# The last stage of a two-layer convolution kernel: which units come first, how far the projection runs ahead, and who issues the last stores

## The chip, the cores and the metric

The kernel runs on one core of one Trainium2 chip. The metric is device time in microseconds (us): the median of 3 executions of the whole kernel. The profile is of one execution; its span counts from the first to the last instruction. A core has five engines that the text names: TensorE (PE, with its weight loads shown apart as PEld), VectorE (DVE), ScalarE (ACT), GpSimd (POOL) and SyncE (SP, which here only issues DMAs). Each takes its own instructions in program order and they meet through semaphores. Results of TensorE land in PSUM; everything else lies in SBUF; x and the output lie in HBM.

## The reference, cut to what matters

The input x is one image of 384 channels by 192 x 192 pixels in float32. Two layers are added to it in turn:

```python
# layer 0: group norm, 1x1 products to q, k, v, 2x2 max, 3x3 depthwise, channel attention, GELU,
#          each pixel repeated to 2x2, 1x1 projection
x = x + _L0_conv_ref(_gn(x), w_qkv, b_qkv, w_dw, b_dw, w_proj, b_proj, temperature, a1, a2, a3, a4)
# layer 1: group norm, sign, a shift along the row that depends on the channel, 1x1 product with signs
x = x + _L1_conv_ref(_gn(x), weight, bias)

def _L1_conv_ref(x, weight, bias):            # cut
    xb, wb = sign(x), sign(weight)
    shifted = ...                             # channel c reads w + dx(c), dx between -3 and 3
    return einsum('bchw,oc->bohw', shifted, wb) + bias
```

The second group norm only decides signs, so of its statistics the kernel needs the mean of each group: `sign(x - mean)`. That mean is a mean over the whole image, so no sign can be taken before layer 0's attention is finished everywhere.

## The kernel before: the parts that matter

The image is worked on in 24 units of 8 rows. One unit of x is a tile of 128 partitions x 3 channel tiles x 1536 pixels, 2304 KB. The results of attention (`chunk`) are kept in SBUF, 4 units to a chunk, 6 chunks. Chunks and units of x share a pool of 8 slots (`big`); two single slots, `early` and `more`, are opened when other data is gone. So as the last stage begins, 6 slots hold chunks and 4 hold units of x. As the projections of a chunk's four units are done, its slot takes a unit.

In the last stage each unit goes through four steps:

- `summed` (`projected`): TensorE multiplies the attention result by the projection weights, 3 float32 matmuls for each of 3 output tiles m; VectorE adds product, bias and x in two instructions (even and odd rows) for each m;
- `signed`: ScalarE takes signs, 6 half-tiles, GpSimd moves some channels to their shifts;
- `finished`: TensorE multiplies the signs by the sign weights, 12 fp8 matmuls for each m; VectorE adds them to x in two instructions for each m;
- `stored`: a DMA to HBM, and into the freed slot the load of a later unit.

```python
    def projected(ps, u, m):
        xt = kept[u]
        o = chunk[u // UC][:, :, u % UC * PPX : (u % UC + 1) * PPX]
        x5 = xt.rearrange("p t (i a j b) -> p t a i j b", a=2, b=2, j=WP)
        for t in range(CT):
            nc.tensor.matmul(ps, wpr[:, t, m * P : (m + 1) * P], o[:, t, :], start=(t == 0), stop=(t == CT - 1))
        yb = ps.rearrange("p (i j) -> p i j", j=WP).unsqueeze(3).to_broadcast([P, PR, WP, 2])
        for r in range(2):
            nc.vector.scalar_tensor_tensor(x5[:, m, r], yb, bpr[:, m : m + 1], x5[:, m, r], ALU.add, ALU.add)
    ...
        with tc.manual_schedule():                       # end of the stage before; FIRST = (19, 18)
            ...
            for m in range(CT):
                projected(pqkv.tile(...)[:, :PPX], FIRST[0], m)
            attention(NAB - 1)
            projected(pqkv.tile(...)[:, :PPX], FIRST[1], 0)
            nc.vector.tensor_reduce(om, osum, AX.X, ALU.add)
            projected(pqkv.tile(...)[:, :PPX], FIRST[1], 1)
            ps = psp.tile([P, P], F32, name="p3ps")[:NG, :1]
            for t in range(CT):
                nc.tensor.matmul(ps, wg1[:, t], om[:, t : t + 1], start=(t == 0), stop=(t == CT - 1))
            nc.vector.tensor_scalar(gm, ps, -1.0 / (GRP * NPX), bg1, ALU.mult, ALU.add)
            projected(pqkv.tile(...)[:, :PPX], FIRST[1], 2)
            ps = psp.tile([P, P], F32, name="p3ps")[:, :CT].unsqueeze(2)
            spread(ps, gm)
            nc.vector.tensor_add(nmean1, nmean0, ps[:, :, 0])          # the mean, negative
    att.close()

    with end:
        more, sp = opened("p5x1", 1), opened("p5s", 1)
        pyp, psp = opened("p5py", 2, space=PSUM), opened("p5ps", 3, space=PSUM)
        ...
        ahead = [*FIRST, NU - 1, *(u for u in order if u // UC == FIRST[0] // UC and u not in FIRST)]
        order = [*ahead, *(u for u in order if u not in ahead)]        # 19, 18, 23, 17, 16, 22, 21, 20, 15, ...

        def signed(i):
            xt, sg = kept[order[i]], signs[i % NSIGN]                  # NSIGN = 3
            for k in range(2 * CT):
                ...
                nc.scalar.activation(..., AF.Sign, bias=nmean1[p, t : t + 1], saturate=False)
                moved(sg, t, h)                                        # GpSimd
                if i > 1 and k == min(2 * (i - 2), CT):
                    stored(i - 2)

        def finished(i, m):
            ...
            for r0 in range(0, UR, 4):
                ps = psp.tile([P, 2, 512], F32, name="l1ps")
                ...                                                    # 6 fp8 matmuls
                nc.vector.scalar_tensor_tensor(blk, ps[:, :, : 2 * W], bl1[:, m : m + 1], blk, ALU.add, ALU.add)
            if i + 2 >= NU:
                nc.sync.dma_start(ov[u, :, m], xt[:, m])

        def stored(i):
            ...
            n = 1 if i < CT else CT
            for t in range(0, CT, n):
                nc.scalar.dma_start(ov[u][:, t : t + n], xt[:, t : t + n])
            if todo:
                v = todo.pop(0)                                        # refill the slot
                for t in range(0, CT, n):
                    nc.sync.dma_start(xt[:, t : t + n], xv[v][:, t : t + n])
                kept[v] = xt

        with tc.manual_schedule():
            v = todo.pop(0)
            kept[v] = unit(v, more, parts=CT)
            for i in range(4):
                for m in range(CT):
                    summed(i, m)
                if i < 2:
                    signed(i)
            for i in range(NU):
                for m in range(CT):
                    if 1 < i < NU - 2:
                        summed(i + 2, m)
                    finished(i, m)
                if i + 2 < NU:
                    signed(i + 2)
```

`manual_schedule` means that each engine gets its instructions in just this order.

Of the kernel before, what the change touches and what calls it, by code (L numbers as in the profile page):

```python
# [10 lines left out]
F32 = mybir.dt.float32  # L11
# [5 lines left out]
ALU = mybir.AluOpType  # L17
# [130 lines left out]
def conv_preact_kernel(ctx: ExitStack, tc: tile.TileContext, a: dict, out: bass.AP):  # L148
# [406 lines left out]
    def opened(name, bufs, **kw):  # L555
        return end.enter_context(tc.tile_pool(name=name, bufs=bufs, reuse_waits="tile", **kw))

    def projected(ps, u, m):

        xt = kept[u]  # L560
        o = chunk[u // UC][:, :, u % UC * PPX : (u % UC + 1) * PPX]
        x5 = xt.rearrange("p t (i a j b) -> p t a i j b", a=2, b=2, j=WP)
        for t in range(CT):
            nc.tensor.matmul(  # L564
                ps,
                wpr[:, t, m * P : (m + 1) * P],
                o[:, t, :],
                start=(t == 0),
                stop=(t == CT - 1),
            )  # L570
        yb = ps.rearrange("p (i j) -> p i j", j=WP).unsqueeze(3).to_broadcast([P, PR, WP, 2])
        for r in range(2):
            nc.vector.scalar_tensor_tensor(x5[:, m, r], yb, bpr[:, m : m + 1], x5[:, m, r], ALU.add, ALU.add)  # L573

    chunk = []
    with ExitStack() as vs:
        wp = vs.enter_context(tc.tile_pool(name="p4w", bufs=1, side="right", reuse_waits="tile"))
        scratch = vs.enter_context(ExitStack())
        p3 = right("p3", stack=scratch)
        vs.enter_context(products_of_x)  # L580
        pool = padded(wp, CT)
        done, steps = 0, None

        def weights(name):
            wl = wp.tile([P, CT, C], F32, name="wl")
            tc.keep_in_program_order(nc.scalar.dma_start(wl, a[name].rearrange("(t p) o -> p t o", p=P)))
            return wl

        def attention(g):

            c, b = divmod(g, CPX // ABLK)
            cols = slice(b * ABLK, (b + 1) * ABLK)
            pss = [po.tile([P, ABLK], F32, name="ops") for _ in range(NP)]
            for t in range(CT):
                for p in range(NP):
                    rows = slice(p * Q, (p + 1) * Q)
                    nc.tensor.matmul(  # L597
                        pss[p][:PAIR],
                        aT[rows, t, p * PAIR : (p + 1) * PAIR],
                        chunk[c][rows, t, cols],  # L600
                        start=(t == 0),
                        stop=(t == CT - 1),
                    )
            for p, ps in enumerate(pss):
                for t in [p] if p < CT else range(CT):
                    src, to = (slice(0, PAIR),) * 2 if p < CT else (slice(t * Q, (t + 1) * Q), slice(PAIR, P))
                    nc.scalar.activation(chunk[c][to, t, cols], ps[src], AF.Gelu, accum_out=osum[to, t, g : g + 1])

        for u in range(NU):
            xt = kept.pop(NU + u) if NU + u in kept else unit(u)  # L610
            if u == NU - 1:
                kept[u] = xt
                for i, f in enumerate(FIRST):
                    kept[f] = unit(f, big if i else early)
            if u % UC == 0:
                chunk.append(big.tile([P, CT, CPX], F32, name="chunk", tag="big"))
            lo, hi = rows(u)
            first = PR * u - 2 + lo
            last = first + hi - lo
            for m in range(CT):  # L620
                parts = []
                for c in range(first // CR, last // CR + 1):
                    r0, r1 = max(first, c * CR), min(last, c * CR + CR - 1)
                    parts.append(
                        (chunk[c][:, m, (r0 - c * CR) * WP : (r1 + 1 - c * CR) * WP], r0 - first, r1 + 1 - r0)
                    )
                qkv_unit(pqkv, xt, u, 2 * CT + m, pool[m], parts)
                if m == 0 and u == UC:

                    wl = weights("w_projG").rearrange("p t (g c) -> p t g c", c=GRP)  # L630
                    tc.keep_in_program_order(nc.vector.tensor_reduce(wg1, wl, AX.X, ALU.add))
                if m == 0 and u == UC + 1:
                    tc.keep_in_program_order(nc.scalar.activation(wb, weights("weightT"), AF.Sign, saturate=False))
                if u == 0 and m == CT - 1:
                    gathered()
                    po = vs.enter_context(tc.tile_pool(name="p4o", bufs=NP, space=PSUM))
                    psp = vs.enter_context(tc.tile_pool(name="p3ps", bufs=1, space=PSUM))
                    bg = psp.tile([P, P], F32, name="p3ps")[:NG, :1]
                    group_sums(bg, bpr.unsqueeze(2))
                    nc.vector.tensor_scalar_mul(bg1, bg, -1.0 / GRP)  # L640
                if u >= TOPK and steps is None:
                    steps = softmaxes(p3, psp)
                if steps:
                    if next(steps, 1):
                        steps = ()
                        scratch.close()
                        early = opened("p5x0", 1)
                elif steps == () and done < NAB - HOLD and (done + 1) * ABLK <= first * WP:
                    attention(done)
                    done += 1  # L650
        with tc.manual_schedule():

            assert done == NAB - HOLD
            for g in range(done, NAB - 1):
                attention(g)
            for m in range(CT):
                projected(pqkv.tile([P, 512], F32, name="qkv")[:, :PPX], FIRST[0], m)
            attention(NAB - 1)
            projected(pqkv.tile([P, 512], F32, name="qkv")[:, :PPX], FIRST[1], 0)
            nc.vector.tensor_reduce(om, osum, AX.X, ALU.add)  # L660
            projected(pqkv.tile([P, 512], F32, name="qkv")[:, :PPX], FIRST[1], 1)
            ps = psp.tile([P, P], F32, name="p3ps")[:NG, :1]
            for t in range(CT):
                nc.tensor.matmul(ps, wg1[:, t], om[:, t : t + 1], start=(t == 0), stop=(t == CT - 1))
            nc.vector.tensor_scalar(gm, ps, -1.0 / (GRP * NPX), bg1, ALU.mult, ALU.add)
            projected(pqkv.tile([P, 512], F32, name="qkv")[:, :PPX], FIRST[1], 2)
            ps = psp.tile([P, P], F32, name="p3ps")[:, :CT].unsqueeze(2)
            spread(ps, gm)
            nc.vector.tensor_add(nmean1, nmean0, ps[:, :, 0])  # L669

    att.close()


    with end:
# [10 lines left out]
            return ts[p, at : at + UR * pitch].rearrange("p (r w) -> p r w", w=pitch)[:, :, :n]  # L685

        order = [u for c in reversed(range(NCH)) for u in reversed(range(c * UC, (c + 1) * UC))]
        ahead = [*FIRST, NU - 1, *(u for u in order if u // UC == FIRST[0] // UC and u not in FIRST)]
        order = [*ahead, *(u for u in order if u not in ahead)]
        left = [UC] * NCH  # L690
        todo = [u for u in order if u not in kept]
# [1 line left out]
        def summed(i, m):  # L693

            u = order[i]
            if i >= len(FIRST):
                projected(pyp.tile([P, PPX], F32, name="yps"), u, m)
            if m < CT - 1:
                return
            left[u // UC] -= 1  # L700
            if not left[u // UC] and todo:
                v = todo.pop(0)
                kept[v] = unit(v)

        def moved(sg, t, h):

# [20 lines left out]
        def signed(i):  # L727

            xt, sg = kept[order[i]], signs[i % NSIGN]
            for k in range(2 * CT):  # L730
# [7 lines left out]
                    saturate=False,  # L738
                )
                moved(sg, t, h)  # L740
                if i > 1 and k == min(2 * (i - 2), CT):
                    stored(i - 2)

        def finished(i, m):
# [3 lines left out]
            for r0 in range(0, UR, 4):  # L748
                ps = psp.tile([P, 2, 512], F32, name="l1ps")
                for j in range(2):  # L750
                    for t in range(CT):
# [4 lines left out]
                            start=(t == 0),  # L756
                            stop=(t == CT - 1),
                        )
                blk = xt[:, m, r0 * W : (r0 + 4) * W].rearrange("p (j n) -> p j n", j=2)
                nc.vector.scalar_tensor_tensor(  # L760
                    blk, ps[:, :, : 2 * W], bl1[:, m : m + 1], blk, ALU.add, ALU.add
                )
            if i + 2 >= NU:
                nc.sync.dma_start(ov[u, :, m], xt[:, m])

        def stored(i):


            u = order[i]
            xt = kept.pop(u)  # L770
            n = 1 if i < CT else CT
            for t in range(0, CT, n):
                nc.scalar.dma_start(ov[u][:, t : t + n], xt[:, t : t + n])
            if todo:
# [6 lines that stand above are left out]
# [6 lines left out]
                    signed(i)  # L787

            for i in range(NU):
                for m in range(CT):  # L790
                    if 1 < i < NU - 2:
                        summed(i + 2, m)
                    finished(i, m)
                if i + 2 < NU:
                    signed(i + 2)
# [72 lines left out]
```

## Time and profile before

| what | value |
|---|---|
| time, median of 3 (lowest, highest) | 2256.28 us (2255.89, 2258.26) |
| span of the profiled execution | 2254.6 us |
| mean granted TensorE clock | 0.968 |
| PE busy over the span | 2090.4 us (93%) |
| DVE busy | 1902.2 us (84%) |
| ACT busy | 819.7 us (36%) |
| POOL busy | 211.3 us (9%) |
| DMA moved | 300.30 MB, mean 133 GB/s |

In the page's picture of 40 slices the first 3 are statistics of x, about 31 are the two passes of layer 0, and the last 5 to 6 are the stage that is changed:

```
PE   1039999999999999999999999999999999999998
DVE  4667888888888888888888888986788888889998
ACT  4542222222222222222222222225333233397885
DMA  9962222232222222222223212105221312279997
```

Each digit is a busy share in tenths. In the last slices PE, DVE and the DMA engines all stand at 9: three resources are near their limit at once there, whereas before it PE stands at 9, DVE at 8 and the DMA at 2. The places where the change acts are the slice where the digits of DMA climb from 2 to 9 and the last one.

### The profile page before, as it was taken

What the parts mean: (1) busy time and instruction counts of PE and PEld (TensorE: products, weight loads), DVE (VectorE), ACT (ScalarE), POOL (GpSimd) and SP (SyncE); (2) the same over time, 40 slices, a digit from 0 to 9 for tenths busy, and PEclk for the clock granted to TensorE, in tenths of its full rate; (3) what the DMA queues carried; (4) which work ended last, traced back from release to release, by engine and by line L of the source; (5) the groups of instructions that cost most, each with busy time, mean ns of one, the idle gap of its engine ahead of it and who ended that gap; (6) DMA issues with size and microseconds to landing.
All of it is one profiled execution on the core that took longest, in us unless ns stands there. A gap on an engine that the chain in (4) does not pass through costs nothing.

```text
span 2254.6 us, 19480 instructions
## 1 busy us (share of the span) xinstructions
PE 2090.4 (93%) x6135; PEld 991.7 (44%) x6135; DVE 1902.2 (84%) x3267; ACT 819.7 (36%) x1418; POOL 211.3 (9%) x338
## 2 busy tenths in 40 slices
PE   1039999999999999999999999999999999999998
PEld 0014444444444444444444444443444444455554
DVE  4667888888888888888888888986788888889998
ACT  4542222222222222222222222225333233397885
POOL 0000000000000000000000000000000000086775
PEclk7559999999999999999999999999999999999999
DMA  9962222232222222222223212105221312279997
GB/s 397 418 277 62 65 64 70 66 105 67 70 63 67 71 73 96 71 67 63 70 67 94 77 35 85 53 11 210 84 84 42 113 55 84 84 296 394 424 425 308
DMA packets 208759, 300.30 MB, mean 133 GB/s; under 512 B 162032, under 2 KB 164880, under 8 KB 208656
## 3 DMA queue, kind: packets, MB, share of 16 engines
q1 hardware_dynamic: 197968, 243.46, 30.5%
q10 hardware_dynamic: 10688, 55.61, 6.0%
q8 instruction: 48, 0.79, 0.1%
q14 instruction: 55, 0.45, 0.1%
HBM read 213.68 MB, written 56.62 MB: 120 GB/s over the span
## 4 chain that ended last, share of the span: by engine, by line
PE 79%; DVE 11%; DMA 6%; ACT 2%; issue 1%; ACTq 0%; POOL 0%; SPq 0%; POOLq 0%; DVEq 0%
PE qkv L331 64%; DMA xt<-in_x_dram 6%; PE l1ps L752 5%; PE yps L564 5%; DVE chunk L356 5%; PE gram L415 3%; DVE pooled L338 2%; PE ops L597 2%; DVE dw L356 1%; ACT signs L733 1%; DVE xt L760 1%; ACT chunk L354 0%; ACT pooled L347 0%; DVE xt L573 0%; DMA small<-in_small_dram 0%
## 5 line engine op out<-in xcount | busy, mean ns | idle before, releaser
L331 PE MATMUL qkv<-xt,wq 128*128 128x512 f32 x3888 | 1684.0, 594 | 4.1 <-DVE pooled L338 3.3
L331 PEld LDWEIGHTS qkv<-xt,wq 128*128 128x128 f32 x3888 | 736.7, 190 | 925.6 <-issue 825.3
L356 DVE SCALAR_TENSOR_TENSOR dw<-pooled,small,dw 128x384 f32<-128x384 f32 (+2 forms) x1152 | 708.7, 615 | 118.8 <-ACT dw L354 93.6
L338 DVE TENSOR_REDUCE pooled<-qkv 128x128 f32<-128x512 f32 x648 | 442.3, 684 | 71.8 <-PE qkv L331 71.5
L356 DVE SCALAR_TENSOR_TENSOR chunk<-pooled,small,chunk 128x384 f32<-128x384 f32 (+3 forms) x696 | 369.7, 545 | 73.2 <-ACT chunk L354 55.5
L358 ACT COPY pooled<-pooled 128x196 f32<-128x196 f32 x207 | 73.7, 356 | 762.6 <-DVE dw L356 542.5
L347 ACT ACTIVATE pooled<-pooled,small 128x384 f32<-128x384 f32 x216 | 133.0, 616 | 405.8 <-DVE pooled L338 389.3
L733 ACT ACTIVATE signs<-xt,nmean 64x1536 fp8e4<-64x1536 f32 x144 | 226.5, 1573 | 47.7 <-PE yps L564 25.6
L752 PE MATMUL l1ps<-signs,wb 128*128 128x384 fp8e4 x864 | 152.6, 326 | 5.4 <-POOL signs L725 5.1
L760 DVE SCALAR_TENSOR_TENSOR xt<-l1ps,small,xt 128x768 f32<-128x768 f32 x144 | 138.8, 1008 | 4.1 <-issue 3.2
L564 PE MATMUL yps<-chunk,wpr 128*128 128x384 f32 x396 | 138.2, 487 | 1.8 <-DVE nmean L669 1.4
L573 DVE SCALAR_TENSOR_TENSOR xt<-yps,small,xt 128x768 f32<-128x768 f32 x132 | 128.0, 1012 | 12.9 <-PE yps L564 5.0
L276 DVE BATCH_NORM_STATS2 room<-xt 128x6 f32<-128x512 f32 x144 | 88.1, 676 | 49.1 <-DMA xt<-in_x_dram 49.1
L227 POOL MEMSET pooled<- 128x196 f32 x9 | 2.4, 265 | 1327.9 <-DVE dw L356 1310.5
L752 PEld LDWEIGHTS <-wb 128*128 128x128 fp8e4 x864 | 83.7, 97 | 78.1 <-issue 19.6
L438 ACT ACTIVATE sq<-dw 128x384 bf16<-128x384 f32 (+2 forms) x144 | 75.3, 523 | 117.5 <-DVE dw L356 117.5
L198 PE MATMUL gsps<-sums,small 128*32 128x2 f32 x6 | 0.5, 196 | 125.0 <-DVE sums L292 125.0
L354 ACT ACTIVATE dw<-pooled,small 128x384 f32<-128x384 f32 (+2 forms) x144 | 100.5, 698 | 2.2
L564 PEld LDWEIGHTS yps<-chunk,wpr 128*128 128x128 f32 x396 | 73.2, 190 | 42.9 <-issue 2.1
L270 ACT ACTIVATE room<-xt 128x1536 bf16<-128x1536 f32 x48 | 71.2, 1483 | 55.8 <-DMA xt<-in_x_dram 55.0
L386 DVE STREAM_TRANSPOSE blocks<-dw 128x384 f32<-128x384 f32 (+1 forms) x144 | 82.0, 569 | 3.4
L711 POOL COPY rest<-signs 9x384 int32<-9x384 int32 (+1 forms) x144 | 72.3, 502 | 70.6 <-ACT signs L733 65.1
(115 smaller groups left out, 629.7 us busy)
## 6 DMA issues: line engine op xcount, KB each, us to landing
xt<-in_x_dram SPq DMA_DIRECT2D x82, 2304.0 KB, 13.8
out_dram<-xt ACTq DMA_DIRECT2D x19, 2304.0 KB, 15.6
room<-blocks SPq DMA_DIRECT2D x736, 36.0 KB, 1.9
xt<-in_x_dram SPq DMA_DIRECT2D x21, 768.0 KB, 9.4
out_dram<-xt ACTq DMA_DIRECT2D x9, 768.0 KB, 8.1
out_dram<-xt SPq DMA_DIRECT2D x6, 768.0 KB, 6.6
wq<-in_w_qkvT_dram ACTq DMA_DIRECT2D x1, 1728.0 KB, 15.1
room<-blocks SPq DMA_DIRECT2D x32, 48.0 KB, 2.0
```

The costliest lines, as they stand in the source:

```text
L276: nc.vector.bn_stats(stats[b][:, t, at : at + 6], xt[:, t, j * 512 : (j + 1) * 512])
L331: nc.tensor.matmul(ps, wq[:, t, m * P : (m + 1) * P], x4[:, t, r0 : r0 + nr, c0 : c0 + ncol], start=(t == 0), stop=(t == CT - 1),)
L338: nc.vector.tensor_reduce(pl[:, 2 + r0 // 2 : 2 + (r0 + nr) // 2, 1 + c0 // 2 : 1 + (c0 + ncol) // 2], ps.rearrange("p (i a j b) -> p i j ...
L347: nc.scalar.activation(new, new, AF.Identity, bias=bq[:, m : m + 1])
L354: nc.scalar.activation(acc2, src, AF.Identity, bias=bdw[:, m : m + 1], scale=wdw[:, m, 0:1])
L356: nc.vector.scalar_tensor_tensor(acc2, src, wdw[:, m, k : k + 1], acc2, ALU.mult, ALU.add)
L386: nc.vector.transpose(to[:, :full], acc[:, : full * P].rearrange("p (k j c) -> p k j c", j=NBP, c=B))
L564: nc.tensor.matmul(ps, wpr[:, t, m * P : (m + 1) * P], o[:, t, :], start=(t == 0), stop=(t == CT - 1),)
L573: nc.vector.scalar_tensor_tensor(x5[:, m, r], yb, bpr[:, m : m + 1], x5[:, m, r], ALU.add, ALU.add)
L733: nc.scalar.activation(rows_of(sg, p, SAT[t] - HSHIFT[t][h]), xt[p, t, :].rearrange("p (r w) -> p r w", w=W), AF.Sign, bias=nmean1[p, t : ...
L752: nc.tensor.matmul(ps[:, j, : 2 * W], wb[:, t, m * P : (m + 1) * P], rows_of(sg, slice(0, P), SAT[t])[:, r0 + 2 * j : r0 + 2 * j + 2], sta ...
L760: nc.vector.scalar_tensor_tensor(blk, ps[:, :, : 2 * W], bl1[:, m : m + 1], blk, ALU.add, ALU.add)
```

## The change

The diff does five things.

1. The first four units of the last stage are 19, 18, 17, 16, all of one chunk, in place of 19, 18, 23, 17. Unit 23 is no longer kept from the stage before; unit 17 is loaded into its slot as soon as that slot is free, and unit 16 into `more`. With these four projected, chunk 4 is used up, and its slot takes unit 23 at once, in three parts.
2. The projection runs three units ahead of `finished` for the units at places 4 to 7 (while i is 1 to 4), nothing is projected at i = 5, and from i = 6 on it runs two units ahead as before.
3. The small steps to the second mean are moved together: the last two tiles of unit 18's projection are split, and their additions on VectorE come after the mean's steps.
4. The last three units, not the last two, are stored one channel tile at a time by SyncE, and the very last tile in two halves; ScalarE issues one store fewer, the one that stood between the signs of the last unit.
5. Unit 3's store and its refill are also in three parts.

It is meant to let the transfers and the signs of the last stage begin earlier, to give TensorE work while it would wait for the first signs, and to shorten what comes after the last matmul.

```diff
+    def projection(ps, u, m, ts=range(CT)):      # the matmuls of `projected`, for some t
+    def added(ps, u, m, r):                      # one of its two additions
...
             if u == NU - 1:
-                kept[u] = xt
                 for i, f in enumerate(FIRST):
                     kept[f] = unit(f, big if i else early)
...
+        kept[FIRST[1] - 1] = unit(FIRST[1] - 1)
         with tc.manual_schedule():
...
             projected(pqkv.tile([P, 512], F32, name="qkv")[:, :PPX], FIRST[1], 0)
             nc.vector.tensor_reduce(om, osum, AX.X, ALU.add)
-            projected(pqkv.tile([P, 512], F32, name="qkv")[:, :PPX], FIRST[1], 1)
+            ys = [pqkv.tile([P, 512], F32, name="qkv")[:, :PPX] for m in range(1, CT)]
+            projection(ys[0], FIRST[1], 1)
+            projection(ys[1], FIRST[1], 2, range(1))
             ps = psp.tile([P, P], F32, name="p3ps")[:NG, :1]
             for t in range(CT):
                 nc.tensor.matmul(ps, wg1[:, t], om[:, t : t + 1], start=(t == 0), stop=(t == CT - 1))
             nc.vector.tensor_scalar(gm, ps, -1.0 / (GRP * NPX), bg1, ALU.mult, ALU.add)
-            projected(pqkv.tile([P, 512], F32, name="qkv")[:, :PPX], FIRST[1], 2)
+            projection(ys[1], FIRST[1], 2, range(1, 2))
             ps = psp.tile([P, P], F32, name="p3ps")[:, :CT].unsqueeze(2)
             spread(ps, gm)
+            projection(ys[1], FIRST[1], 2, range(2, CT))
+            added(ys[0], FIRST[1], 1, 0)
             nc.vector.tensor_add(nmean1, nmean0, ps[:, :, 0])
+            added(ys[0], FIRST[1], 1, 1)
+            for r in range(2):
+                added(ys[1], FIRST[1], 2, r)
...
-        ahead = [*FIRST, NU - 1, *(u for u in order if u // UC == FIRST[0] // UC and u not in FIRST)]
+        ahead = [*FIRST, *(u for u in order if u // UC == FIRST[0] // UC and u not in FIRST)]
...
-                kept[v] = unit(v)
+                kept[v] = unit(v, parts=CT if i < CT + 1 else 1)
...
-                if i > 1 and k == min(2 * (i - 2), CT):
+                if 1 < i < NU - 1 and k == min(2 * (i - 2), CT):
                     stored(i - 2)
...
+                if (i, m) == (NU - 1, CT - 1):
+                    nc.sync.dma_start(ov[u, :, m, px], xt[:, m, px])
-            if i + 2 >= NU:
+            if i + 3 >= NU and (i, m) != (NU - 1, CT - 1):
                 nc.sync.dma_start(ov[u, :, m], xt[:, m])
...
-            n = 1 if i < CT else CT
+            n = 1 if i < CT + 1 else CT
...
             for i in range(NU):
+                ahead = range(1, 5), range(6, NU - 2)
                 for m in range(CT):
-                    if 1 < i < NU - 2:
-                        summed(i + 2, m)
+                    for r, k in zip(ahead, (3, 2)):
+                        if i in r:
+                            summed(i + k, m)
                     finished(i, m)
```

## The prediction

> **What bounds the kernel now.** I read three views in this order: the table of stretches over the last stage, to see where an engine is idle at all; the instructions of each engine in order of time at the two ends of the stage, to see what ended each idle time; and the DMA issues at the very end.
>
> The stretches have start and end in us, their length, busy time (and count) of PE, PEld, DVE, ACT and POOL, the granted clock, the DMA share and GB/s.
>
> ```profile
> 1957.00:1970.00 13.00, 10.82 (x58) 5.40 (x57) 12.21 (x16) 4.17 (x13) 1.86 (x3) 1.00 0.46 181
> 1970.00:1983.00 13.00, 12.62 (x40) 6.74 (x41) 10.04 (x11) 12.80 (x9) 9.54 (x15) 1.00 0.01 2
> 1983.00:2002.00 19.00, 15.21 (x86) 8.66 (x85) 15.21 (x17) 18.70 (x13) 16.41 (x25) 1.00 0.77 285
> 2002.00:2220.00 218.00, 217.72 (x1004) 126.87 (x1003) 209.51 (x223) 180.52 (x115) 158.69 (x230) 1.00 0.99 409
> 2220.00:2235.00 15.00, 14.99 (x75) 8.67 (x74) 14.67 (x16) 11.28 (x8) 11.35 (x17) 1.00 0.39 159
> 2235.00:2248.00 13.00, 10.46 (x63) 5.88 (x61) 11.57 (x13) 3.15 (x2) 3.05 (x5) 1.00 0.93 381
> 2248.00:2255.00 7.00, 0.00 (x0) 0.00 (x0) 0.00 (x0) 0.00 (x0) 0.00 (x0) 0.56 0.74 304
> ```
>
> From 2002 to 2235 TensorE is idle for 0.29 us in all: the middle of the stage is bound by TensorE, with VectorE at 96% and the DMA at 0.99 close behind. Nothing in the change removes a matmul, so 233 us of it can't shrink. What can shrink is the 45 us before 2002 and the 20 us after 2235. In the first, DMA is at 0.01 for 13 us and TensorE loses 3.8 us of 19; in the second no engine but the DMA works for the last 7 us.
>
> The start, engine by engine (start, duration, what, idle before and its releaser); PE first, then DVE, then ACT:
>
> ```profile
> 1969.91 2.50 PE L564 MATMUL yps<-chunk,wpr 128*128 128x384 f32 x7 [1.37 <-DVE nmean L669]
> ...
> 1991.21 5.74 PE L752 MATMUL l1ps<-signs,wb 128*128 128x384 fp8e4 x34 [2.19 <-POOL signs L725]
> ...
> 2000.80 1.80 PE L752 MATMUL l1ps<-signs,wb 128*128 128x384 fp8e4 x10 [1.59 <-POOL signs L725]
> ```
>
> ```profile
> 1969.68 0.14 DVE L669 TENSOR_TENSOR nmean<-nmean,p3ps 128x3 f32<-128x3 f32 x1
> 1972.12 3.88 DVE L573 SCALAR_TENSOR_TENSOR xt<-yps,small,xt 128x768 f32<-128x768 f32 x4 [2.30 <-PE yps L564]
> ...
> 1984.52 5.63 DVE L760 SCALAR_TENSOR_TENSOR xt<-l1ps,small,xt 128x768 f32<-128x768 f32 x6
> 1992.12 5.88 DVE L760 SCALAR_TENSOR_TENSOR xt<-l1ps,small,xt 128x768 f32<-128x768 f32 x6 [1.97 <-issue]
> ```
>
> ```profile
> 1969.91 17.56 ACT L733 ACTIVATE signs<-xt,nmean 64x1536 fp8e4<-64x1536 f32 x11 [5.29 <-issue]
> ```
>
> TensorE twice waits for signs. They start at 1969.91, right after the mean, and 12 half-tiles at 1.6 us take 19.2 us, while TensorE needs only about 6 us per unit to use them up as long as it has no projection between.
>
> The end: ACT, then PE, DVE and SP:
>
> ```profile
> 2235.21 0.38 ACTq L773 DMA_DIRECT2D out_dram<-xt  x1
> 2235.71 3.17 ACT L733 ACTIVATE signs<-xt,nmean 64x1536 fp8e4<-64x1536 f32 x2 [2.14 <-PE l1ps L752]
> ```
>
> ```profile
> 2241.03 5.74 PE L752 MATMUL l1ps<-signs,wb 128*128 128x384 fp8e4 x34 [1.31 <-POOL signs L725]
> ```
>
> ```profile
> 2241.94 5.88 DVE L760 SCALAR_TENSOR_TENSOR xt<-l1ps,small,xt 128x768 f32<-128x768 f32 x6 [1.21 <-issue]
> ```
>
> ```profile
> 2237.06 11.13 SPq L764 DMA_DIRECT2D out_dram<-xt  x6
> ```
>
> ScalarE's last two signs stand behind the store of place 21, which itself waits for VectorE to finish that unit (2235.2). So the signs come late, TensorE loses 1.31 us and VectorE 1.21. And that store is 2304 KB in one piece: after 2235.2 three whole units, 3 x 2.36 = 7.08 MB, still have to go out, and at the 415 to 425 GB/s seen there this takes 17 us. VectorE is done at 2247.8; the span ends at 2254.6, 6.8 us later.
>
> **What the Trainium skill says.** "Perfetto Trace Analysis", section Optimization Strategy, advises to find the gaps on the engine that one optimizes, within one regime, and the semaphore that ends each; that is the method here, and the trace has just the gaps of 2.19, 1.59 and 1.31 us to offer. The same page, section Sequencer Loop, has each sequencer read one instruction after the other; the trace agrees that a DMA issue that waits holds up what follows it on ACT (sign at 2235.71 right after the issue at 2235.21). "DMA: Bandwidth & Descriptors", section Issuing engines are not separate DMA queues, says that DMAs of different engines share the same 16 DMA engines; so moving place 21's store from ACT to SP gives no bandwidth, only an earlier issue. Its section on the anatomy of one DMA gives a fixed part of about 2 us beside the bytes (for another issuing path); here the quickest of the 768 KB stores landed after 3.4 us, of which 0.786 MB at 425 GB/s are 1.85, so the fixed part is 1.55, and I use that.
>
> **The change part by part.** Some of this is read from the changed program's own list of instructions with their semaphores, which shows order and waits and no times.
>
> *Mean earlier.* Before, between the sum over `osum` (1965.05) and the mean (1969.68) VectorE does four additions of 0.97 us and TensorE three matmuls in one piece. After, one addition and one matmul lie between. The sum's matmuls still end at 1965.65; `gm` can follow at 1965.9 and not 1967.01; the spreading matmuls (0.82 us) then run from 1966.3 to 1967.1, and the mean comes at about 1967.4. Signs begin near 1967.55 rather than 1969.91: 2.35 us earlier.
>
> *But the first projection of the new stage is not earlier.* In the changed program its PSUM tile waits for VectorE's last addition to unit 18, because it takes over those banks. That addition comes now after the mean: three additions from 1967.4 end at 1970.3, so the matmuls start at 1970.45, 0.55 us later than the 1969.91 of before. The 12 additions for places 2 and 3 then take the same pattern (two at a time, 4.3 us for four, bound by the two buffers): the last ends at 1985.15 rather than 1984.6, and `finished(0)` starts on TensorE at about 1983.0 (before: 1982.46). Its signs are ready: 1967.55 + 6 x 1.6 + 2.1 for GpSimd = 1979.3.
>
> *The wait for signs is filled.* Unit 1's signs are complete at 1967.55 + 19.2 + 2.1 = 1988.9. TensorE ends `finished(0)` at 1983.0 + 6.3 = 1989.3, and has `summed(4, 0)`, 1.94 us, before it needs them. Unit 2's: ScalarE's queue stands at the store of place 0 until VectorE has finished that (1990.9), so these signs end at 1991.1 + 5 x 1.6 + 2.1 = 2001.2; TensorE comes to them after `finished(1)` and three projections, at 1989.3 + 11.7 + 1.9 = 2002.9. Neither wait is left, so 2.19 + 1.59 + the 0.28 of 2052 = 4.1 us are won and 0.55 lost: 3.5 us. On VectorE the same count gives 3.1: its steps up to the first addition of place 2's `finished` are 1985.15 + 5.8 + 1.9 + 5.8 = 1998.6, before 2001.73. I take 3.4.
>
> *Loads.* Unit 17's load starts when TensorE last reads unit 23, near 1950, with the DMA free. Unit 23's second load waits for the last projection of place 3, at 1983.0; its three parts land at about 1986.5, 1988.5 and 1990.5, and VectorE wants the first at 1990.9. From then on the number of bytes is that of before: 24 stores and 20 loads, 104 MB, 244 us at 425 GB/s, against 257 us until VectorE's end. So this part moves transfers and adds none after 1983; the extra load lies in the time at 0.01. Gain of its own: nothing. It is there so that projecting three ahead has a unit to work on.
>
> *Nothing at i = 5.* There ScalarE has 9.5 us of signs for 5.9 us of TensorE's, but runs up to two units ahead by then and is bound only by the three sign buffers. I count 0.
>
> *The end.* Place 21's store leaves ACT: the last signs come 2.1 us earlier, so the gaps of 1.31 on PE and 1.21 on DVE go; gain 1.2. With three units stored in nine parts, each goes out as VectorE ends it, one part of 1.85 us of transfer for 1.96 us of VectorE, so there is no backlog. With T as VectorE's end: the part issued at T - 1.96 lands at T + 1.5, the first half of the last tile at T + 2.4, the second at T + 3.3; with 0.3 us for the end of the program, T + 3.6 in place of T + 6.8. Gain 3.2.
>
> Sum: 3.4 + 1.2 + 3.2 = 7.8 us. 2256.3 - 7.8 = 2248.5 us, 0.35%.
>
> **The rivals.** *The load comes too late.* With three units ahead a unit of x is held one step (11.7 us) longer, while only 5 slots hold units until chunk 5 is used up. A slot's refill must wait for the store: for place 6 the store is issued after sign 3 of place 3, near 2004, and the first part of the new unit lands at about 2012, needed at 2014.5; place 7 likewise, 2 to 3 us of room. For it: the DMA is at 0.99 in the middle, and before the change VectorE already waited 2.3 us for a load near 2047. Against it: refills in parts, and before the change TensorE never felt that wait. If each of three units were late by 2 to 3 us, the time would be 2254 to 2257, no gain. *VectorE becomes the bound.* It needs 12 x 0.97 = 11.6 us for a unit and TensorE 11.7; any wait that hits VectorE can't be made up. That would take 1 to 2 us off the gain: 2250. *The DMA is behind at the end.* If the stores of places 20 and 21 collide, the tail keeps 2 of its 6.8 us more: 2250.5. *It goes better:* if starting loads and signs earlier also removes VectorE's small waits around 2047, and the tail ends at T + 3, the time is 2246.
>
> **Range and chances.** The two ends are separate gains, 4.4 at the end (rather sure, it follows from the issue order) and 3.4 at the start (less sure). Losing the whole start gives 2252; both with 1 to 2 us more gives 2246. Executions of before spread over 2.4 us. So 2248.5 us, 2245.5 to 2252.5. 2% would be 45 us, more than all the idle time of this stage, so within 2% is almost certain: 0.98, and 0.01 on each side.
>
> **What would show it.** Right: signs begin about 2.3 us earlier against the start of unit 19's projection, `yps` a little later than before with a wait for an addition; no wait for GpSimd's signs on PE of over 0.5 us; the DMA at work again before 1985 (before the change: after 1986.5); at the end no wait on PE for signs, and 3.5 to 4 us from VectorE's last instruction to the end. Wrong: a wait of VectorE for a load between 1998 and 2045, idle TensorE there, or a last store that lands 5 us or more after VectorE.

## The result, and the profile after

| kernel | median, us (lowest to highest) | span of the profiled execution |
|---|---|---|
| before | 2257.27 (2255.89 to 2259.51) | 2254.6 |
| after | 2248.51 (2248.30 to 2248.76) | 2246.8 |

The ratio is 0.996, with a 95% interval of 0.9943 to 0.9978: the change makes the kernel 0.4% faster, by 5 to 13 us. The two traces differ by 7.8 us; the medians differ by 8.8, because the trace of before is of an execution of 2256.42 us and others of that kernel were slower.

The table of stretches of the kernel after (start and end, length, busy time of PE, PEld, DVE, ACT and POOL, granted clock, DMA share, GB/s):

```profile
1970.00:1983.00 13.00, 12.43 (x38) 6.74 (x39) 9.80 (x12) 12.80 (x9) 11.05 (x17) 1.00 0.01 2
1983.00:2002.00 19.00, 18.99 (x95) 11.14 (x93) 18.26 (x20) 16.03 (x11) 13.93 (x21) 1.00 0.95 348
2002.00:2220.00 218.00, 218.00 (x1015) 127.05 (x1015) 211.28 (x224) 182.58 (x118) 161.91 (x235) 1.00 0.97 404
2220.00:2235.00 15.00, 14.99 (x81) 8.69 (x80) 14.78 (x17) 12.50 (x8) 11.27 (x16) 1.00 0.85 347
2235.00:2248.00 13.00, 6.21 (x38) 3.46 (x36) 7.26 (x8) 0.00 (x0) 0.00 (x0) 0.88 0.80 325
```

In the second row TensorE is busy for all of the 19 us, where it lost 3.8 before. The DMA now carries 0.85 between 2220 and 2235, where it had 0.39: the stores of place 21 go out there. TensorE's instructions after, in order of time (idle before and releaser in brackets):

```profile
1967.00 0.91 PE L562 MATMUL qkv<-chunk,wpr 128*128 128x384 f32 x2
1970.19 4.11 PE L562 MATMUL yps<-chunk,wpr 128*128 128x384 f32 x12 [2.27 <-DVE xt L574]
...
1982.74 6.24 PE L767 MATMUL l1ps<-signs,wb 128*128 128x384 fp8e4 x36
1988.81 2.10 PE L562 MATMUL yps<-chunk,wpr 128*128 128x384 f32 x6
1990.74 2.13 PE L767 MATMUL l1ps<-signs,wb 128*128 128x384 fp8e4 x12
```

The first bracket is the wait for the projection's PSUM banks, released by VectorE's addition (L574). From 1982.74 on no line has a bracket up to the last matmul: each of the three waits for signs is gone. ScalarE after:

```profile
1967.35 20.75 ACT L748 ACTIVATE signs<-xt,nmean 64x1536 fp8e4<-64x1536 f32 x13 [2.95 <-issue]
1986.76 4.04 ACTq L791 DMA_DIRECT2D out_dram<-xt  x3
1990.85 6.37 ACT L748 ACTIVATE signs<-xt,nmean 64x1536 fp8e4<-64x1536 f32 x4 [2.75 <-DVE xt L776]
```

Signs begin at 1967.35 instead of 1969.91. After 13 of them ScalarE stands for 2.75 us, because its queue is at the three issues of place 0's store, which wait for VectorE. VectorE and then SP at the end:

```profile
2229.16 13.10 DVE L776 SCALAR_TENSOR_TENSOR xt<-l1ps,small,xt 128x768 f32<-128x768 f32 x14
```

```profile
2241.36 1.46 SPq L780 DMA_DIRECT2D out_dram<-xt  x2
```

VectorE goes through its last 14 additions without a gap and ends at 2242.26; the two halves of the last tile are issued from 2241.36 to 2242.82, land 3.6 us after their issue, and the span ends at 2246.8, 4.5 us after VectorE (before: 6.8).

The same additions in the kernel before began with this group:

```profile
2233.25 7.48 DVE L760 SCALAR_TENSOR_TENSOR xt<-l1ps,small,xt 128x768 f32<-128x768 f32 x8
```

The first two of the eight, like the first two of the 14, belong to place 21. Where the 7.8 us came from, by the two traces: VectorE ends place 21 at 2231.1 and not 2235.2, 4.1 us (0.2 of it were won before the stage began); from there to its last instruction 11.2 us and not 12.65, 1.4 us; from there to the end 2.2 us.

### The profile page after: what moved, and what is told of

Read it like the earlier page. It is cut to its first block, busy times and chain, and to the rows that moved or that the text cites. A ratio compares the mean times of both kernels' runs of the same rounds, so it can differ in the third digit from the quotient of the medians.

```text
span 2246.8 us, 19512 instructions
## 1 busy us (share of the span) xinstructions
PE 2091.4 (93%) x6135; PEld 994.1 (44%) x6135; DVE 1903.1 (85%) x3267; ACT 819.6 (36%) x1418; POOL 211.3 (9%) x338
## 4 chain that ended last, share of the span: by engine, by line
PE 83%; DVE 9%; DMA 5%; ACT 1%; issue 0%; SPq 0%; ACTq 0%; DVEq 0%
PE qkv L331 66%; PE l1ps L767 6%; PE yps L562 6%; DMA xt<-in_x_dram 5%; DVE chunk L356 4%; PE gram L415 3%; PE ops L604 2%; DVE pooled L338 2%; DVE dw L356 1%; DMA wq<-in_w_qkvT_dram 1%; DVE xt L574 1%; PE wgps L284 0%; ACT room L270 0%; PE qkv L562 0%; ACT chunk L354 0%
## 5 line engine op out<-in xcount | busy, mean ns | idle before, releaser
L574 DVE SCALAR_TENSOR_TENSOR xt<-yps,small,xt 128x768 f32<-128x768 f32 x132 | 128.2, 1013 | 10.9 <-PE yps L562 4.4
```

## The experiments

| run | median, us (lowest to highest) | ratio to before, 95% interval |
|---|---|---|
| end only, on the kernel before | 2254.30 (2252.14 to 2257.45) | 0.9985 (0.9979 to 0.9992) |
| all but the end | 2252.53 (2252.16 to 2253.85) | 0.9973 (0.9964 to 0.9982) |
| place 21's store left on ScalarE | 2253.09 (2251.99 to 2253.99) | 0.9979 (0.9971 to 0.9988) |
| two ahead throughout | 2255.30 (2252.18 to 2256.56) | 0.9990 (0.9982 to 0.9998) |
| two ahead, place 0's store issued later | 2249.69 (2248.48 to 2250.97) | 0.9963 (0.9950 to 0.9975) |
| mean in its old order | 2248.30 (2248.00 to 2248.51) | 0.9962 (0.9949 to 0.9974) |
| mean alone, on the kernel before | 2260.43 (2256.40 to 2261.71) | 1.0009 (1.0002 to 1.0015) |
| first four units of before | 2263.43 (2262.31 to 2265.02) | 1.0026 (1.0017 to 1.0036) |
| loads in one piece | 2250.28 (2249.56 to 2252.03) | 0.9968 (0.9955 to 0.9980) |
| PSUM pools swapped | 2245.67 (2244.94 to 2246.11) | 0.9949 (0.9937 to 0.9962) |
| PSUM pools swapped, mean in its old order | 2248.12 (2247.05 to 2248.58) | 0.9956 (0.9943 to 0.9970) |

Each ratio is to executions of the kernel before that were taken together with that run; their medians were 2257.27, 2258.38 and 2257.82 us. The kernel after was not executed again with them, so a difference to its 2248.51 of under about 1 us is not shown to be one.

**The end by itself.** On the kernel before:

```diff
-                if i > 1 and k == min(2 * (i - 2), CT):
+                if 1 < i < NU - 1 and k == min(2 * (i - 2), CT):
                     stored(i - 2)
...
+                if (i, m) == (NU - 1, CT - 1):
+                    nc.sync.dma_start(ov[u, :, m, px], xt[:, m, px])
-            if i + 2 >= NU:
+            if i + 3 >= NU and (i, m) != (NU - 1, CT - 1):
                 nc.sync.dma_start(ov[u, :, m], xt[:, m])
```

> The kernel before with only the end of the change: places 21 to 23 stored tile by tile by SyncE, the last tile in halves, no store on ScalarE between the signs of the last unit. Theory (the two ends are separate gains): the wait of 1.31 us for the last signs goes, VectorE's last instruction ends 1.2 to 1.4 us earlier against the end of place 21, and the span ends about 4.5 us after it instead of 6.8; together 3.5 to 3.8 us, a time near 2253. Rival (the end is bound by the DMA and only an earlier start of all transfers shortens it): under 1 us.

VectorE's last additions of this run:

```profile
2234.85 13.10 DVE L761 SCALAR_TENSOR_TENSOR xt<-l1ps,small,xt 128x768 f32<-128x768 f32 x14
```

The wait for the last signs is gone, and from VectorE's end, 2247.95, to the end of the span (2252.5) it is 4.55 us: the same two gains as in the whole change. The median fell by 3.0 us and not 3.5 to 3.8; in the profiled execution VectorE waited 4.8 us for loads (3.1 in the profiled execution of before) and TensorE 1.5 us for VectorE because of it. So with the old start late loads can reach TensorE, which my theory had at nearly nothing; in the trace of before only 0.28 us of them did, and how often it is more is not shown.

**The change without the end.** On the kernel after, the three places of the diff above go back:

```diff
-                if 1 < i < NU - 1 and k == min(2 * (i - 2), CT):
+                if i > 1 and k == min(2 * (i - 2), CT):
...
-                if (i, m) == (NU - 1, CT - 1):
-                    nc.sync.dma_start(ov[u, :, m, px], xt[:, m, px])
-            if i + 3 >= NU and (i, m) != (NU - 1, CT - 1):
+            if i + 2 >= NU:
```

> The changed kernel with the end of before (place 21 stored by ScalarE in one piece between the signs of the last unit, whole tiles, two units by SyncE). Theory (two separate gains): 3.7 us come back, a time near 2252.2, with the wait of 1.3 us for the last signs and 6.8 us from VectorE's last instruction to the end. Rival (with the transfers begun earlier the DMA is less behind at the end, so the end matters less): under 2 us more.

2252.53, 4.0 us more than after, near what the theory said. The last additions stand in two pieces again:

```profile
2229.84 7.48 DVE L775 SCALAR_TENSOR_TENSOR xt<-l1ps,small,xt 128x768 f32<-128x768 f32 x8
2238.54 5.88 DVE L775 SCALAR_TENSOR_TENSOR xt<-l1ps,small,xt 128x768 f32<-128x768 f32 x6 [1.22 <-issue]
```

VectorE ends at 2244.4 and the span at 2251.3, 6.9 us later. The two ends add up.

**One store of the end.** On the kernel after, only place 21 goes back to ScalarE in one piece; the halves of the last tile stay.

```diff
-                if 1 < i < NU - 1 and k == min(2 * (i - 2), CT):
+                if i > 1 and k == min(2 * (i - 2), CT):
...
-            if i + 3 >= NU and (i, m) != (NU - 1, CT - 1):
+            if i + 2 >= NU and (i, m) != (NU - 1, CT - 1):
```

> The changed kernel, but the store of place 21 stays with ScalarE in one piece between the signs of the last unit; the last tile still goes out in halves. Theory (both parts of the gain at the end hang on this one store: the late signs and the 7.08 MB left after place 21): the wait of 1.3 us for the last signs is back and three whole units go out after place 21, so nearly all of the 3.7 us come back, 2251.5 to 2252.5. Rival (the halved last tile gives most of it): under 1.5 us more than 2248.5.

2253.09: all of the gain at the end is lost. The wait of 1.3 us is back, and the span ends 6.9 us after VectorE although the last tile goes out in halves. This one store is what the end is about; the halves help nothing while other stores are in front of them. The run moves the store to ScalarE and joins its three parts at once. The late signs come from its place in ScalarE's queue; how much of the time after VectorE comes from the one piece is not separated.

**Two ahead throughout.**

```diff
-                ahead = range(1, 5), range(6, NU - 2)
                 for m in range(CT):
-                    for r, k in zip(ahead, (3, 2)):
-                        if i in r:
-                            summed(i + k, m)
+                    if 1 < i < NU - 2:
+                        summed(i + 2, m)
```

> The changed kernel, but projecting two units ahead throughout as before (first four units, early refill, mean and end as changed). Theory (the gain at the start is the wait for signs that three-ahead fills): TensorE reaches the signs of place 2 at about 1996.6 and they are ready only at about 2001, since ScalarE's queue stands at the store of place 0; so a new wait of about 4.3 us, the time near 2252.8, and no gain left at the start. Rival (the gain comes from transfers that begin earlier): as the changed kernel, within 1 us of 2248.5.

TensorE of this run around the signs of place 2, and then stretches of 4 us:

```profile
1996.63 0.33 PE L767 MATMUL l1ps<-signs,wb 128*128 128x384 fp8e4 x1
1997.37 0.32 PE L767 MATMUL l1ps<-signs,wb 128*128 128x384 fp8e4 x1 [0.41 <-POOL signs L735]
2001.18 3.36 PE L767 MATMUL l1ps<-signs,wb 128*128 128x384 fp8e4 x10 [3.49 <-POOL signs L740]
2004.34 3.17 PE L562 MATMUL yps<-chunk,wpr 128*128 128x384 f32 x6
2007.34 2.13 PE L767 MATMUL l1ps<-signs,wb 128*128 128x384 fp8e4 x12
```

```profile
1996.00:2000.00 4.00, 1.28 (x5) 0.47 (x4) 1.94 (x2) 3.95 (x3) 3.10 (x6) 0.96 1.01 353
2000.00:2004.00 4.00, 2.82 (x9) 1.29 (x9) 1.02 (x1) 3.92 (x4) 3.76 (x5) 0.50 1.00 407
2004.00:2008.00 4.00, 4.00 (x12) 2.32 (x11) 1.48 (x2) 3.95 (x3) 3.54 (x7) 0.69 1.02 419
```

The wait is there, 3.49 + 0.41 us, and the signs come when the theory said. But the median is 2.5 us above the 2252.8 expected: from the end of the wait on TensorE's clock was granted at 0.50, and the projection matmuls of one output tile took 3.17 us instead of 2.10. One execution of this kernel came to 2252.18 us, with a mean clock of 0.970; the other twelve lay between 2255.1 and 2256.6, at 0.968 or 0.969. The rival, that early transfers alone bring the gain, falls.

**The store in ScalarE's queue.** The run before, and in `signed`:

```diff
-                if 1 < i < NU - 1 and k == min(2 * (i - 2), CT):
+                if 1 < i < NU - 1 and k == (2 * CT - 1 if i == 2 else min(2 * (i - 2), CT)):
```

> Two units ahead throughout, as in the run that lost the gain at the start, but with the store of place 0 issued by ScalarE after the last sign of place 2 and not after the first. Theory (two thirds of that loss are ScalarE's queue standing at the store, and the half clock after it): the signs of place 2 are ready near 1998.6, TensorE waits about 2 us for them and not 4, the clock stays at full, and the time is near 2250.5 with a small spread. Rival (the clock falls by itself in that stretch): half clock again and 2253 or more.

2249.69, 5.6 us better than the run it differs from by one line. In its trace TensorE waits for no signs, where I had expected about 2 us:

```profile
1969.80 7.74 PE L562 MATMUL yps<-chunk,wpr 128*128 128x384 f32 x18 [2.28 <-DVE xt L574]
...
1997.95 2.13 PE L767 MATMUL l1ps<-signs,wb 128*128 128x384 fp8e4 x12
```

TensorE comes to the signs of place 2 at 1997.95, and GpSimd's last copy for them ends at 1997.8. But this execution came there late: in the first line the clock was granted at 0.62 (1970 to 1974), and from the mean's first matmul to the first sign product 19.3 us passed, against 17.6 in the kernel after. At full clock TensorE would have come 1.7 us earlier and waited about 1.5 us (an estimate from these numbers). The run before has the same slow start and still waited 3.9. So the wait that three-ahead fills was made mostly, by about 2.4 of 3.9 us, by the place of an issue in ScalarE's queue; moving that issue is almost as good (1.2 us more than after).

**The mean.** The kernel after with the old order of the mean's steps, and the kernel before with the new order alone (the same diff the other way round):

```diff
-            ys = [pqkv.tile([P, 512], F32, name="qkv")[:, :PPX] for m in range(1, CT)]
-            projection(ys[0], FIRST[1], 1)
-            projection(ys[1], FIRST[1], 2, range(1))
+            projected(pqkv.tile([P, 512], F32, name="qkv")[:, :PPX], FIRST[1], 1)
...
-            projection(ys[1], FIRST[1], 2, range(1, 2))
+            projected(pqkv.tile([P, 512], F32, name="qkv")[:, :PPX], FIRST[1], 2)
...
-            projection(ys[1], FIRST[1], 2, range(2, CT))
-            added(ys[0], FIRST[1], 1, 0)
             nc.vector.tensor_add(nmean1, nmean0, ps[:, :, 0])
-            added(ys[0], FIRST[1], 1, 1)
-            for r in range(2):
-                added(ys[1], FIRST[1], 2, r)
```

> The changed kernel with the steps to the second mean in their old order. Theory: signs start 2.3 us later but the first projection 0.5 us earlier; the signs of place 1 come 0.5 to 0.8 us after TensorE asks for them, so the time is 0 to 0.6 us more, near 2249. Rival (the earlier mean is what brings the gain at the start): 2 to 2.4 us more, near 2250.8.

> The kernel before with only the steps to the second mean moved together. Theory (the earlier mean alone moves the waits but wins nothing): no wait for the signs of place 1, but TensorE then stands about 4 us before the signs of place 2, which are behind the store of place 0 in ScalarE's queue; and since a wait over 3.5 us was followed by 6 us at half clock in the run with two ahead, the time is 2256 to 2260, not better than before. Rival (the signs are the bound at the start, and their 2.35 us go straight into the time): near 2255.

The old order in the kernel after gives 2248.30 against 2248.51, no difference. The new order alone on the kernel before gives 2260.43, slower than the 2258.38 of before beside it, by 0.2 to 1.5 per mille. TensorE in that run:

```profile
1970.25 4.11 PE L562 MATMUL yps<-chunk,wpr 128*128 128x384 f32 x12 [2.28 <-DVE xt L574]
...
2001.02 1.80 PE L766 MATMUL l1ps<-signs,wb 128*128 128x384 fp8e4 x10 [3.49 <-POOL signs L739]
```

The wait of 2.19 us for the signs of place 1 has gone, but that for place 2 has grown from 1.59 us to 3.49. Late loads reach TensorE with another 1.8 us (0.3 in the trace of before). Signs that start 2.4 us earlier are worth nothing by themselves.

**The first four units.** On the kernel after:

```diff
             if u == NU - 1:
+                kept[u] = xt
...
-        kept[FIRST[1] - 1] = unit(FIRST[1] - 1)
...
-        ahead = [*FIRST, *(u for u in order if u // UC == FIRST[0] // UC and u not in FIRST)]
+        ahead = [*FIRST, NU - 1, *(u for u in order if u // UC == FIRST[0] // UC and u not in FIRST)]
```

> The changed kernel with the first four units of before (19, 18, 23, 17; unit 23 kept, 17 in the late slot), but still projecting three ahead. Theory (the new order is needed because three ahead asks for the unit of place 4 while there are only four slots): that unit now goes into the slot of place 0, which is stored first; VectorE waits for it some 4 us near 1991, 8 us for place 5 and 4 us for place 7, and the time is 2258 to 2266. Rival (the order brings little, the loads are quick enough): within 1.5 us of 2248.5.

```profile
1995.67 1.94 DVE L574 SCALAR_TENSOR_TENSOR xt<-yps,small,xt 128x768 f32<-128x768 f32 x2 [5.43 <-PE l1ps L767]
...
2016.58 1.94 DVE L574 SCALAR_TENSOR_TENSOR xt<-yps,small,xt 128x768 f32<-128x768 f32 x2 [9.40 <-DMA xt<-in_x_dram]
```

These are VectorE's additions for places 4 and 5. The first gap is 5.4 us (the profile names a sign product, which these additions do not read; of the things they do wait for the load is the late one, issued from 1990.0 on and with a median of 6.3 us to landing), the second is 9.4, and TensorE loses 10.3 us in two waits for VectorE. After both waits some matmuls ran at half clock, which makes 3.4 us more (an estimate from their durations); together that is the 13.7 us by which the span is longer than after. 2263.43, slower than before. Three ahead needs the early fifth slot, and the new order of units is what gives it.

**Loads in one piece.** On the kernel after:

```diff
-                kept[v] = unit(v, parts=CT if i < CT + 1 else 1)
+                kept[v] = unit(v)
...
-            n = 1 if i < CT + 1 else CT
+            n = 1 if i < CT else CT
```

> The changed kernel with unit 23's second load, and the store and refill of place 3, in one piece each. Theory (the three parts only let VectorE begin with the first tile): the load lands near 1991, when VectorE asks for it, and TensorE's lead hides what is missing; 0 to 1 us more than 2248.5. Rival (the parts are what keeps three ahead supplied): VectorE waits 3 us or more and the time is over 2250.5.

2250.28, 1.8 us more, between theory and rival. VectorE waits 2.26 us for unit 23, until 1992.8, and 2.66 us for a load, until 2071.0, and the latter reaches TensorE with 1.4 us. The lead of TensorE hides the first late load, not the later one.

**The banks.** On the kernel after:

```diff
-        pyp, psp = opened("p5py", 2, space=PSUM), opened("p5ps", 3, space=PSUM)
+        psp, pyp = opened("p5ps", 3, space=PSUM), opened("p5py", 2, space=PSUM)
```

> The changed kernel with the two PSUM pools of the last stage opened in the other order, so that the projection's two banks lie over banks that are free earlier and no longer over those of unit 18's last projection. Theory (the wait of 2.27 us before the first projection is one for these banks and lies on the path): TensorE starts it near 1967.9, goes on without idle time but for about 0.3 us for the signs of place 1, and the time falls by 1.9 to 2.1 us to about 2246.5. Rival (the loads are the next bound): VectorE waits for loads between 2000 and 2045 instead, and under 0.7 us is won.

```profile
1966.95 0.91 PE L562 MATMUL qkv<-chunk,wpr 128*128 128x384 f32 x2
1967.70 4.03 PE L562 MATMUL yps<-chunk,wpr 128*128 128x384 f32 x12
1971.99 4.11 PE L562 MATMUL yps<-chunk,wpr 128*128 128x384 f32 x12 [0.26 <-DVE xt L574]
```

The wait of 2.27 us before `yps` is gone, the projection starts 2.49 us earlier and the span is 2.5 us shorter; 2245.67, 2.8 us better than after (1.9 to 2.1 expected, and the 0.3 us for signs did not come), and better than both kernels by more than their executions scatter. This is the version to keep.

With the old order of the mean's steps on top of it:

> The kernel with the PSUM pools swapped, but with the steps to the second mean in their old order. Theory (the earlier mean was worth nothing in the changed kernel because TensorE stood before the projection's banks for just as long; with the banks free the signs are the next bound): TensorE waits 2 to 2.7 us for the signs of place 1 and the time is 2247.6 to 2248.6. Rival (the mean's place does not matter with three ahead, as the run with the old mean showed): as the swapped kernel, within 0.6 us of 2245.7.

```profile
1990.90 1.80 PE L760 MATMUL l1ps<-signs,wb 128*128 128x384 fp8e4 x10 [1.59 <-POOL signs L733]
```

2248.12: TensorE waits for signs again (1.59 us, less than the 2 to 2.7 expected), its projection starts 0.45 us later (1968.15), and 2.4 us of the swap's 2.8 are lost. So the earlier mean is worth 2.4 us once the banks are free, and nothing while they are not.

## Why the prediction was right, step by step

The time, 2248.5, was met, the three terms of the sum less exactly: by the traces the start gave 0.7 us more than predicted, the signs at the end 0.2 more, the last stores 1.0 less. That these errors cancel to the hundredth is luck.

- **Mean earlier, 2.35 us.** Signs start 2.56 us earlier, of which 0.17 is the earlier arrival at the stage. Right.
- **First projection 0.55 us later.** It is 0.28 later, 0.45 after taking off the same 0.17. Right, with the wait on VectorE's addition that was foreseen. That this wait undoes the earlier mean altogether follows from the two runs on the mean and the two on the banks; I had put only the 0.55 in the sum.
- **Waits for signs filled, 3.4 us at the start.** No wait is left, and the start brought 4.1 us between the traces, 0.2 of it before the stage. The cause stands by the run with two ahead; that ScalarE's queue at place 0's store delays the signs of place 2 was in the working, and the run with the later store shows that it is most of that wait (about 2.4 of 3.9 us).
- **Loads: no gain of their own, room of 2 to 3 us.** Half right. In the kernel after VectorE waits 0.3 us for a load in all. But with loads in one piece a late load reaches TensorE with 1.4 us and the time is 1.8 us longer, so without the parts the room is not there; and the end alone, on the old start, shows 1.5 us of the same kind.
- **Nothing at i = 5: 0.** Right: TensorE's line shows no gap there.
- **End: 1.2 and 3.2 us.** The first came to 1.4. The second to 2.2: the term that was mis-sized is the time from VectorE's last instruction to the end, 4.5 us and not 3.6 (nor the 3.5 to 4 named as the sign of being right). The second half is issued at 2242.3, right at VectorE's end; it lands 3.6 us later, where I had 3.3, no sooner than a whole tile does in the median (3.4), and from there to the end it is 0.9 us where I had 0.3.
- **Rivals.** A load that comes too late was real for the old order of units (2263) and is just avoided by the new one. VectorE as the bound, and a DMA behind at the end, did not occur.

## What to carry to other kernels

A wait on one engine is often made by the place of an instruction in another engine's queue: here one DMA issue on ScalarE, which waits for VectorE, stood before signs that TensorE needed, at the start and at the end of the stage; ask of every issue on a computing engine what stands behind it. Two waits that end at nearly the same time hide each other: an earlier mean was worth nothing until the projection's PSUM banks were free as well, and then 2.4 us. Where a stage opens new pools, look which of the old tiles their banks lie over, and lay the first one needed over the one that is free first.

## What the runs showed of the hardware

A wait of TensorE can cost more than its length. In the run with two ahead the clock stood at half for about 6.8 us around and after the wait of 3.49 us (worked out from 0.96, 0.50 and 0.69 in stretches of 4 us), 5.3 us of them after its end. The Trainium skill, "TensorE: Matmul & The Clock Gate", section What's actually happening, says that the clock falls to half after an idle window of about 3.4 us and that the window runs freely; the 0.50 agrees. The wait's length alone doesn't decide it: the run with only the mean moved has the same 3.49 us in its profile and a clock of 1.00 after it.

A shorter wait can do it too. Eight traces have a wait of 2.27 or 2.28 us before the first projection. Four of them (two ahead, the store issued later, without the end, place 21 on ScalarE) show half clock after it, for about 3.4 us each: 0.62 and 0.95 in the stretches from 1970 to 1978 of the run with the later store. From the mean's first matmul to the first sign product they take 19.3 us. The other four, the kernel after among them, show 1.00 and take 17.6. The kernel after and the run without the end have the same instructions up to there, so executions of one kernel can differ by 1.7 us at this place. The four at half clock are those that came to the mean's matmuls earliest (1963.41 to 1964.74; the others 1964.94 to 1965.24), which would fit a window that runs freely; no run tests it. How often half clock meets the kernel before, whose executions scattered over 3.6 us against 0.5 of the kernel after, no profile here shows; it stays open.
